# A deep-interest ranking network on one core: a sixth tile by address in two of three steps of history, a root on VectorE, categories as products of ones and zeros, and one norm for both parts of a layer

## The chip, the cores and the metric

The kernel runs on one core of one Trainium2 chip. A core has five engines, each with its own instruction queue: TensorE (PE; PEld is its loading of weights), VectorE (DVE), ScalarE (ACT), GpSimd (POOL) and SyncE (SP). SP, ACT and POOL also issue DMA transfers, and 16 DMA engines carry them. A profile writes SPq or ACTq for what such a queue issues. The metric is the time of one execution on the device in microseconds, less is better, taken as the median of several.

## The reference

There are 16,384 samples. For each, 200 items of history (`r_hist`, 200 x 16384 indices), one candidate item, one category and one user are looked up in tables of 64 float32 each.

```python
u = u_emb[user]; it = i_emb[item]; c = c_emb[cate]; h = i_emb[hist]
feat = concat([h, it, h - it, h * it])                  # 200 x 16384 x 256
a = dice(feat @ au_W1 + au_b1, au_alpha, axis=1)        # 36 units
cur = sum(w * h, axis=0), with w = a @ au_W2 + au_b2    # over the 200
z = dice(concat([u, it, c, cur]) @ W1 + b1, alpha1, axis=0)
z = dice(z @ W2 + b2, alpha2, axis=0)
return z @ W3 + b3
```

`dice(x)` is `x * (p + alpha * (1 - p))`, where `p` is the sigmoid of `x` normalised by its mean and variance. In the attention the mean runs over all samples of one step l of the history; in the head it runs over all samples.

## The kernel before

The 16,384 samples are 128 tiles of 128. Sixteen tiles make a column c, so one step l of the history has eight columns (ND = 8), and the program goes through k = 8 l + c. The 200 l are four passes of a loop whose body is 45 l written out, and then 20 l written out (`BODY`, `LPB`).

For each k, `fetch` (helper `gather`, L123) has POOL gather 16 tiles of rows, one indirect DMA of 128 rows each, into one of five buffers `rows`. Some tiles come another way. In the columns SIDES = (1, 3, 4, 5, 6, 7) the last tile is copied row by row with addresses: `load_addresses` (L145) brings the indices into `addr`, VectorE multiplies them by the row's bytes (L148), and `rows_by_address` loads 16 or 20 addresses at a time into registers (L293) and issues one DMA of 256 bytes for each row (L301), half on SP's queue and half on ACT's. The rows land in one of three tiles `side`, and the semaphore `landed` counts them. Column 5 (`SOMETIMES`) does so only when l is divisible by 3; otherwise POOL gathers that tile, with indices from `load_side_ids` (L142). So of three l one has six tiles by address (96 rows per k) and two have five (80 rows per k). `place` makes ACT wait for `landed`, clear it, and copy `side` into `rows` (L352).

The order within a k is written by hand in `step`: gathers for k; ACT's move of the units of k-2 out of `px` (L339); at the end of an l the moments (L363 on, with the square root on ACT at L170 and the reciprocal on VectorE at L171); ACT's sigmoid for k-9 (`gate`, L328; LAG = 9); `place` for k-1; the rows by address for k; then for k-1 VectorE's four transposes (L156) and TensorE's products, and VectorE's work for k-2, k-1 and k-9 (L344, L360, L331, L335, L336). A new l opens with the load of indices for the next one on SP (L136).

Ahead of the loop the candidate items are gathered by POOL, 128 gathers. After it, `head_fetch` gathers categories and users, 256 gathers; `head_layer` makes the first layer's products and moves its 64 and 16 units out separately (L486, L488). `head_moments` runs once for each part and once for the second layer, each with a square root on ACT; then come the two further layers and the output.

```python
for k in range(n * ND):
    l, c = divmod(k, ND)
    if c == 0 and l + 1 < end:
        load_hist_ids((l + 1) % IDX, l0 + l + 1)
```

Of the kernel before, what the change touches and what calls it, by code (L numbers as in the profile page):

```python
# [28 lines left out]
LOAD = 20  # L29
# [5 lines left out]
def din_kernel(  # L35
# [76 lines left out]
    ids = [make(f"ids{i}", P, NT, dt=I32) for i in range(3)]  # L112
# [17 lines left out]
    def load_ids(t, v):  # L130
        nc.sync.dma_start(t[:, :NC], columns(v))
        for s in range(NS):
            nc.sync.dma_start(t[:, NC + s : NC + s + 1], col(v[(NC + s) * P : (NC + s + 1) * P]))

# [9 lines left out]
    def load_addresses(i, l):  # L144
        nc.sync.dma_start(addr[i], r_hist[ds(l, 1), NC * P :])  # L145
# [21 lines left out]
    def scale_and_shift(mean, var, rstd, shift):  # L167
        n = mean.shape[0]
        std = small.tile([P, 1], F32, tag="std", name="std")
        nc.scalar.activation(std[:n], var, AF.Sqrt, bias=eps[:n])  # L170
        nc.vector.reciprocal(rstd, std[:n])  # L171
        nc.vector.scalar_tensor_tensor(shift, mean, -1.0, rstd, ALU.mult, ALU.mult)

    eps = make("eps", P, 1)
# [14 lines left out]
    def attention_weights():  # L189
        nc.vector.memset(eps, EPS)  # L190
# [45 lines left out]
    def head_weights():  # L236
# [3 lines left out]
        for e in range(2):  # L240
            for g in range(2):
                r, d = quarter(e, g), ts(e, S)
                nc.sync.dma_start(w1a[r, :, ts(g, ZA)], w1[d, :, :ZA])
                nc.sync.dma_start(w1b[r, :, ts(g, ZB)], w1[d, :, ZA:])
        for g in range(2):
            nc.sync.dma_start(w2a[ts(g, ZA), g * ZA : g * ZA + Z2], W2[:ZA])
# [20 lines left out]
    flat = i_emb.rearrange("v d -> (v d)").bitcast(U8)  # L267

# [4 lines left out]
    def tiles_by_address(l):  # L273

        round_, i = divmod(l, EACH)
        first = round_ * (EACH * (NS - 1) + 1) + i * (NS - 1) + (i > 0)
        return first, [j for j, c in enumerate(SIDES) if has_side(l * ND + c)]

    def rows_by_address(k):
        l, s = divmod(k, ND)  # L280
        first, tiles = tiles_by_address(l)
        n = len(tiles) * P // ND // 2
        loads = -(-n // LOAD)
        for i, (engine, issue) in enumerate(
            ((mybir.EngineType.SP, nc.sync), (mybir.EngineType.Activation, nc.scalar))
        ):
            r0, end = (2 * s + i) * n, (2 * s + i + 1) * n
            while r0 < end:
                many = min(end - r0, -(-n // loads))
                at0 = tiles[r0 // P] * P + r0 % P  # L290
                while tiles[(r0 + many - 1) // P] * P + (r0 + many - 1) % P != at0 + many - 1:
                    many -= 1
                _, at = nc.values_load_multi_w_load_instructions(  # L293
                    addr[l % 3][:, at0 : at0 + many],
                    engines=(engine,), min_val=0, max_val=ROW * (V - 1),
                    skip_runtime_bounds_check_because="the DMA checks the address against the table",
                )
                for r, a in enumerate(at, r0):
# [9 lines left out]

    def await_rows(m):
        if m in keys:  # L310
            fence = nc.scalar.wait_ge(landed[m % 3], 16 * P)
            tc.declare_fence(fence.ins, group=keys.pop(m))
            nc.scalar.sem_clear(landed[m % 3])

    def has_side(k):
        l, c = divmod(k, ND)
        return c in SIDES and (c != SOMETIMES or l % EACH == 0)
# [28 lines left out]
    def place(k):  # L346
        if has_side(k):
            l, c = divmod(k, ND)
            first, tiles = tiles_by_address(l)
            m = first + tiles.index(SIDES.index(c))  # L350
            await_rows(m)
            nc.scalar.copy(rows[k % ROWS][:, TD - 1], side[m % 3])  # L352
# [30 lines left out]
    def step(k, last=None):  # L383
# [12 lines left out]
        if has(k - LAG):  # L396
            gate(k - LAG)
        if has(k - 1):
            place(k - 1)
        if has(k):  # L400
            rows_by_address(k)
        if has(k - 1):
# [5 lines left out]
        if has(k - LAG):  # L408
# [3 lines left out]
    def steps(l0, n, end):  # L412
        for k in range(n * ND):
            l, c = divmod(k, ND)
            if c == 0 and l + 1 < end:
                load_hist_ids((l + 1) % IDX, l0 + l + 1)
                if (l + 1) % EACH:
                    load_side_ids((l + 1) % IDX, l0 + l + 1)
            if c == 2 and l + 1 < end:
                load_addresses((l + 1) % 3, l0 + l + 1)  # L420
            if c == 4 and l + 1 < end:
                scale_addresses((l + 1) % 3)
            step(k)

    with tc.manual_schedule():
        load_ids(ids[0], r_item)
        load_hist_ids(0, 0)
        load_addresses(0, 0)
        load_ids(ids[1], r_cate)
        load_ids(ids[2], r_user)  # L430
        nc.gpsimd.iota(lanes, pattern=[[1, P]], base=P, channel_multiplier=-1)
        attention_weights()
        for t in (*hT, *xs, *side, hm):
            nc.vector.memset(t, 0.0)
        for t in curT:
# [7 lines left out]
        scale_addresses(0)  # L443
        layer(px, [(blk_m, hm)])

        for c in range(ND + 1):
            if c < ND:
                for n in range(TD):
                    j = column(c, n)
                    gather(rows[c % ROWS], ids[0][:, j : j + 1], n, i_emb)  # L450
            if c:
                transpose(itT[c - 1], rows[(c - 1) % ROWS])
        nc.vector.memset(rows[-1 % ROWS], 0.0)
# [13 lines left out]
    def measure_head(i, j, t):  # L467
        for h in range(2):
            nc.vector.bn_stats(zst[i][:, 2 * j + h, :], t[:, ts(h, CH)])

    def head_fetch(k, j):
        c, u = divmod(j, 2)
        for n in range(TD):
            i = column(c, n)
            gather(rows[k % ROWS], ids[1 + u][:, i : i + 1], n, (c_emb, u_emb)[u])

    def head_layer(j):
        c, u = divmod(j, 2)
        if u == 0:
# [121 lines left out]
```

## Time and profile before

| | |
|---|---|
| median of 10 runs | 51,398.7 us (51,284.0 to 51,432.4) |
| the profiled execution | 51,313.9 us, span 51,312.1 us |
| POOL busy | 23,568.2 us (46%), 24,922 instructions |
| PE busy / PEld busy | 20,767.9 us (40%) / 8,519.6 us (17%) |
| DVE busy | 15,101.6 us (29%) |
| ACT busy | 4,417.8 us (9%) |
| rows by address | 68,288 on SP, 68,288 on ACT |
| gathers of history rows | 24,533 on POOL |

How to read it: issuing a DMA and loading a register are not counted as busy, so SP has no busy time of its own and ACT's is small; what these queues do is seen in the time line and in the waits. In a line of a group, the name left of the arrow is written and those right of it are read; after the bar stand the busy time, the mean of one instruction in ns, and the idle time ahead of them with what ended it. Times of POOL are rough.

### The profile page before, as it was taken

What the parts mean: (1) busy time and instruction counts of PE and PEld (TensorE: products, weight loads), DVE (VectorE), ACT (ScalarE), POOL (GpSimd) and SP (SyncE); (2) the same over time, 40 slices, a digit from 0 to 9 for tenths busy, and PEclk for the clock granted to TensorE, in tenths of its full rate; (3) what the DMA queues carried; (4) which work ended last, traced back from release to release, by engine and by line L of the source; (5) the groups of instructions that cost most, each with busy time, mean ns of one, the idle gap of its engine ahead of it and who ended that gap; (6) DMA issues with size and microseconds to landing.
All of it is one profiled execution on the core that took longest, in us unless ns stands there. A gap on an engine that the chain in (4) does not pass through costs nothing. (4 is left out here: it accounts for less than half of the span.)

```text
span 51312.1 us, 423966 instructions
## 1 busy us (share of the span) xinstructions
PE 20767.9 (40%) x38856; PEld 8519.6 (17%) x38856; DVE 15101.6 (29%) x18955; ACT 4417.8 (9%) x4941; POOL 23568.2 (46%) x24922
## 2 busy tenths in 40 slices
PE   3444444443444444444444444444444444434444
PEld 1111111111111111111111111111111111111111
DVE  2222222232222222222222222222222222222223
ACT  0000000000000000000000000000000000000001
POOL 5444444444444444444444444444444444444444
PEclk6666666676666666666676666666666666666667
DMA  1000000001000000000000000000000001000000
GB/s 19 18 17 17 18 17 17 17 17 18 17 18 17 17 18 17 17 17 17 17 18 17 17 17 18 17 17 17 17 17 18 17 17 18 17 17 17 18 17 17
DMA packets 1130924, 894.71 MB, mean 17 GB/s; under 512 B 729024, under 2 KB 729024, under 8 KB 1127896
## 3 DMA queue, kind: packets, MB, share of 16 engines
q0 software_dynamic: 797344, 818.07, 9.1%
q1 hardware_dynamic: 193112, 31.56, 0.3%
q10 hardware_dynamic: 137440, 17.76, 0.2%
q14 instruction: 2722, 22.30, 0.1%
q8 instruction: 306, 5.01, 0.0%
HBM read 865.10 MB, written 0.13 MB: 17 GB/s over the span
## 5 line engine op out<-in xcount | busy, mean ns | idle before, releaser
L123 POOL DMA_INDIRECT rows<-in_L_rec_i_emb,idx x24400 | 23078.7, 946 | 27336.3 <-DVE hT L156 19722.4
L161 PE MATMUL ph<-hT,unit 128*128 128x512 f32 x6404 | 5955.1, 1085 | 29876.1 <-DVE hT L156 29344.8
L335 DVE SCALAR_TENSOR_TENSOR wb<-wb,au_bias,hT 128x1024 f32<-128x1024 f32 x1609 | 2079.7, 1293 | 22888.2 <-remote 19196.7
L161 PEld LDWEIGHTS ph<-hT,unit 128*128 128x128 f32 x6404 | 1797.9, 311 | 32935.8 <-DVE hT L156 32140.7
L156 DVE STREAM_TRANSPOSE hT<-rows 64x512 f32<-64x512 f32 x6404 | 4516.7, 705 | 9048.8 <-ACT rows L352 8894.5
L339 ACT ACTIVATE xs<-px,au_bias 128x1024 f32<-128x1024 f32 x1602 | 1785.0, 1114 | 45250.8 <-issue 40079.8
L161 PE MATMUL px<-hT,blk_h 128*128 128x512 f32 x6404 | 4020.2, 715 | 403.2 <-ACT xs L339 211.1
L161 PE MATMUL px<-itT,blk_i 128*128 128x512 f32 x6404 | 3423.3, 617 | 0.0
L161 PE MATMUL wb<-xs,blk_x 128*128 128x512 f32 x6436 | 3294.0, 593 | 48.2 <-DVE curT L336 45.4
L161 PE MATMUL wb<-y,blk_p 128*128 128x512 f32 x6436 | 3294.6, 593 | 36.4 <-issue 19.5
L161 PE MATMUL px<-hm,blk_m 128*128 128x512 f32 x6408 | 3013.0, 592 | 71.1 <-remote 71.1
L344 DVE BATCH_NORM_STATS2 st<-xs 128x6 f32<-128x512 f32 x3204 | 2061.6, 686 | 2065.7 <-ACT xs L339 1611.2
L360 DVE TENSOR_TENSOR hm<-ph,itT 128x1024 f32<-128x1024 f32 x1601 | 1958.0, 1223 | 1725.2 <-PE ph L161 1162.2
L161 PEld LDWEIGHTS px<-hT,blk_h 128*128 128x128 f32 x6404 | 1601.0, 252 | 2890.7 <-issue 2528.8
L336 DVE TENSOR_TENSOR curT<-wb,curT 128x1024 f32<-128x1024 f32 x1609 | 1970.0, 1224 | 54.8
L331 DVE TENSOR_TENSOR y<-pg,xs 128x1024 f32<-128x1024 f32 x1609 | 1954.0, 1214 | 12.6 <-issue 10.3
L328 ACT ACTIVATE pg<-xs,sh,rs 128x1024 f32<-128x1024 f32 x1609 | 1934.1, 1202 | 28.4 <-DVE y L331 13.9
L161 PEld LDWEIGHTS px<-itT,blk_i 128*128 128x128 f32 x6404 | 1391.7, 217 | 1963.0 <-issue 1963.0
L161 PEld LDWEIGHTS wb<-xs,blk_x 128*128 128x128 f32 x6436 | 1224.1, 190 | 1593.7 <-issue 1544.4
L161 PEld LDWEIGHTS wb<-y,blk_p 128*128 128x128 f32 x6436 | 1224.7, 190 | 1582.5 <-issue 1559.2
L161 PEld LDWEIGHTS px<-hm,blk_m 128*128 128x128 f32 x6408 | 1218.0, 190 | 1606.1 <-issue 1533.8
L352 ACT COPY rows<-side 128x64 f32<-128x64 f32 x1068 | 251.3, 235 | 682.0 <-DMA side<-in_L_rec_i_emb 588.5
(155 smaller groups left out, 2148.1 us busy)
## 6 DMA issues: line engine op xcount, KB each, us to landing
side<-in_L_rec_i_emb SPq DMA_DIRECT2D x68288, 0.2 KB
side<-in_L_rec_i_emb ACTq DMA_DIRECT2D x68288, 0.2 KB
rows<-in_L_rec_i_emb,idx POOLq DMA_INDIRECT x24400
idx<-in_r_hist SPq DMA_DIRECT2D x200, 61.0 KB
addrs<-in_r_hist SPq DMA_DIRECT2D x200, 3.0 KB
sidx<-in_r_hist SPq DMA_DIRECT2D x133, 0.5 KB
rows<-in_L_rec_i_emb,sidx POOLq DMA_INDIRECT x133
rows<-in_L_rec_i_emb,ids POOLq DMA_INDIRECT x128
```

What stands on the lines that cost most here:

```text
L123: nc.gpsimd.indirect_dma_start(out=dst[:, n, :], out_offset=None, in_=table, in_offset=bass.IndirectOffsetOnAxis(ap=ids, axis=0),)
L156: nc.vector.transpose(by_tile(dst[ts(e, D)], i), of[ts(i, D), :, ts(e, S)])
L161: nc.tensor.matmul(dst[:, ts(i, CH)], lhsT, rhs[:, ts(i, CH)], start=(first and j == 0), stop=(last and j == len(pairs) - 1), skip_group_c ...
L328: nc.scalar.activation(pg, xs[k % XR], AF.Sigmoid, bias=shifts[i], scale=rstds[i])
L331: nc.vector.tensor_mul(y, pg, xs[k % XR])
L335: nc.vector.scalar_tensor_tensor(wb, wb, au_bias2, hT[k % LAG], ALU.add, ALU.mult)
L336: nc.vector.tensor_add(curT[k % ND], wb, curT[k % ND])
L339: nc.scalar.activation(xs[k % XR], px, AF.Identity, bias=au_bias)
L344: nc.vector.bn_stats(stats[l % 3][:, 2 * c + i, :], xs[k % XR][:, ts(i, CH)])
L352: nc.scalar.copy(rows[k % ROWS][:, TD - 1], side[m % 3])
L360: nc.vector.tensor_mul(hm, ph, itT[k % ND])
```

## The change

- Column 5 comes by address in two of three l (`MOST = 2`) in place of one, which makes 17 tiles by address in three l where there were 16. Registers are loaded with up to 24 addresses at a time (`LOAD`). In a step, ACT's share of the rows is issued in two parts, one ahead of its sigmoid and one behind it.
- The wait for landed rows, the clearing and the copy go from ACT to VectorE (`place_tile`).
- One over the root is found on VectorE by three steps of refinement from a shifted bit pattern; ACT has no square root any more.
- Six tiles of the candidate items, and five of the users, come by address as well (`ask_all`). Categories are not gathered: ahead of the loop, for each half column, VectorE compares category numbers with the numbers of 125 table rows at a time, TensorE multiplies the table by these ones and zeros, ACT moves the result out and stores it in DRAM, and the end loads it back by one DMA on SP per column.
- At the end the user and category parts are two calls of `head_layer` per column, both parts of the first layer are normalised in one pass (`start_moments`, `end_moments`), halves are moved out one by one, part of the scaling goes to ACT, and the first output is sent after the seventh column.

```diff
-LOAD = 20
+MOST = 2
+LOAD = 24
+SPLIT = 0.5
...
-        n = mean.shape[0]
-        std = small.tile([P, 1], F32, tag="std", name="std")
-        nc.scalar.activation(std[:n], var, AF.Sqrt, bias=eps[:n])
-        nc.vector.reciprocal(rstd, std[:n])
...
+        nc.vector.tensor_scalar_add(v, var, EPS)
+        nc.vector.tensor_single_scalar(h.bitcast(I32), v.bitcast(I32), 1, ALU.logical_shift_right)
+        nc.vector.tensor_scalar(
+            rstd.bitcast(I32), h.bitcast(I32), -1.0, float(0x5F375A00), ALU.mult, ALU.add
+        )
+        for _ in range(3):
+            if n == 1:
+                nc.vector.scalar_tensor_tensor(h, rstd, v, rstd, ALU.mult, ALU.mult)
...
+            nc.vector.tensor_scalar(h, h, -0.5, 1.5, ALU.mult, ALU.add)
+            nc.vector.tensor_mul(rstd, rstd, h)
...
-                nc.sync.dma_start(w1a[r, :, ts(g, ZA)], w1[d, :, :ZA])
-                nc.sync.dma_start(w1b[r, :, ts(g, ZB)], w1[d, :, ZA:])
+                for f in (slice(0, 2), slice(3, 4)):
+                    nc.sync.dma_start(w1a[r, f, ts(g, ZA)], w1[d, f, :ZA])
+                    nc.sync.dma_start(w1b[r, f, ts(g, ZB)], w1[d, f, ZA:])
...
+            nc.sync.dma_start(w1a[ts(g, D), 2, ts(g, ZA)], w1[:, 2, :ZA])
+            nc.sync.dma_start(w1b[ts(g, D), 2, ts(g, ZB)], w1[:, 2, ZA:])
...
-        first = round_ * (EACH * (NS - 1) + 1) + i * (NS - 1) + (i > 0)
+        first = round_ * (EACH * (NS - 1) + MOST) + i * (NS - 1) + min(i, MOST)
...
+    queues = ((mybir.EngineType.SP, nc.sync), (mybir.EngineType.Activation, nc.scalar))
+    def shares(n, s, split):
+        many = round(n * split)
+        runs = []
+        for r0, end in ((s * n, s * n + many), (s * n + many, (s + 1) * n)):
+            loads = -(-(end - r0) // LOAD)
+            at = [r0 + (end - r0) * i // loads for i in range(loads + 1)]
+            runs.append(list(zip(at, at[1:])))
+        return runs
...
+    def ask(queue, runs, first, tiles, at, table):
+        engine, issue = queues[queue]
...
+        for r0, end in runs:
             while r0 < end:
...
-                _, at = nc.values_load_multi_w_load_instructions(
-                    addr[l % 3][:, at0 : at0 + many],
-                    engines=(engine,), min_val=0, max_val=ROW * (V - 1),
+                _, loaded = nc.values_load_multi_w_load_instructions(
...
+    def ask_hist(k, queue, some):
+        l, s = divmod(k, ND)
+        first, tiles = tiles_by_address(l)
+        runs = shares(len(tiles) * P // ND, s, SPLIT)[queue]
+        ask(queue, runs[some], first, tiles, addr[l % 3], i_emb)
+    def ask_all(s, split, first, n, at, table):
+        for queue, runs in enumerate(shares(NS * P // ND, s, split)):
+            runs = [(r0, min(end, n * P)) for r0, end in runs if r0 < n * P]
+            ask(queue, runs, first, range(n), at, table)
...
         if m in keys:
-            fence = nc.scalar.wait_ge(landed[m % 3], 16 * P)
+            fence = nc.vector.wait_ge(landed[m % 3], 16 * P)
             tc.declare_fence(fence.ins, group=keys.pop(m))
-            nc.scalar.sem_clear(landed[m % 3])
+            nc.vector.sem_clear(landed[m % 3])
...
-        return c in SIDES and (c != SOMETIMES or l % EACH == 0)
+        return c in SIDES and (c != SOMETIMES or l % EACH < MOST)
...
-            m = first + tiles.index(SIDES.index(c))
-            await_rows(m)
-            nc.scalar.copy(rows[k % ROWS][:, TD - 1], side[m % 3])
...
+    def place_tile(k, m):
+        await_rows(m)
+        nc.vector.tensor_copy(rows[k % ROWS][:, TD - 1], side[m % 3])
+    def fetch_all(k, c, ids, table):
+        for n in range(TD - (c in SIDES)):
+            j = column(c, n)
+            gather(rows[k % ROWS], ids[:, j : j + 1], n, table)
...
                 moments((k - 2) // ND)
-        if has(k - LAG):
+        if has(k):
+            ask_hist(k, 0, slice(None))
+            ask_hist(k, 1, slice(0, 1))
+        if k - LAG not in weighed:
             gate(k - LAG)
+        if has(k):
+            ask_hist(k, 1, slice(1, None))
         if has(k - 1):
             place(k - 1)
-        if has(k):
-            rows_by_address(k)
...
-                if (l + 1) % EACH:
+                if (l + 1) % EACH >= MOST:
                     load_side_ids((l + 1) % IDX, l0 + l + 1)
...
+    def order_categories():
+        nc.scalar.dma_start(table, c_emb.rearrange("(b p) d -> p b d", p=PB))
+        for c in range(ND):
...
...
+    def spread_categories(q):
+        c, i = divmod(q, 2)
+        half = cs[c][ts(i, D)].rearrange("p n -> (p n)")
+        nc.scalar.dma_start(spread[q % SPREAD], half.partition_broadcast(PB))
+    def pick_categories(q):
+        for b in range(NB):
+            ones = xs[(q * NB + b) % XR][:PB]
+            nc.vector.tensor_scalar(
+                ones, spread[q % SPREAD], values[:PB, b : b + 1], None, ALU.is_equal
+            )
+            for g in range(2):
+                nc.tensor.matmul(
+                    bank[q % 8][ts(g, D)], table[:, b], ones[:, ts(g, CH)],
+                    start=b == 0, stop=b == NB - 1, skip_group_check=True,
+                )
+        nc.scalar.copy(
+            stages[q % 4].rearrange("p (n t) -> p n t", t=S),
+            bank[q % 8].rearrange("p (t n) -> p n t", n=TD),
+        )
+    def store_categories(q):
+        c, i = divmod(q, 2)
+        nc.scalar.dma_start(catT[c][:, ts(i, CH)], stages[q % 4])
...
     with tc.manual_schedule():
-        load_ids(ids[0], r_item)
+        nc.sync.dma_start(ids[0], columns(r_item))
+        load_addresses(2, r_item.rearrange("(o b) -> o b", o=1))
+        order_categories()
         load_hist_ids(0, 0)
...
+        nc.sync.dma_start(ids[1], columns(r_user))
         nc.gpsimd.iota(lanes, pattern=[[1, P]], base=P, channel_multiplier=-1)
+        for q in range(SPREAD - 1):
+            spread_categories(q)
...
+        scale_addresses(2)
+        nc.vector.memset(hm, 0.0)
+        for t in (*hT[SPREAD:], *curT[1:]):
+            nc.scalar.copy(t, hm)
+        for c in range(ND + 1):
+            if c < ND:
+                fetch_all(c, c, ids[0], i_emb)
+                ask_all(c, 0.56, -NS, NS, addr[2], i_emb)
+                for q in (2 * c, 2 * c + 1):
+                    pick_categories(q)
+                    if q + SPREAD - 1 < HALVES:
+                        spread_categories(q + SPREAD - 1)
+                    if q:
+                        store_categories(q - 1)
+            if c == 0:
+                attention_weights()
+                scale_addresses(0)
+            if c:
+                if c - 1 in SIDES:
+                    place_tile(c - 1, SIDES.index(c - 1) - NS)
+                transpose(itT[c - 1], rows[(c - 1) % ROWS])
+        store_categories(HALVES - 1)
...
+        for t in xs:
+            nc.scalar.copy(t, hm)
+        for t in (*hT[:SPREAD], *side, curT[0], rows[-1 % ROWS]):
             nc.vector.memset(t, 0.0)
...
+    def start_moments(key, j, n, i, same):
...
+        nc.vector.bn_aggr(mv[:, j], zst[i].rearrange("p c s -> p (c s)"))
+        nc.tensor.matmul(leading(pg, j, 1), same, mv[:, j, 0:1], start=True, stop=True)
+    def end_moments(key, sames):
...
+        for j, same in enumerate(sames):
+            nc.tensor.matmul(leading(wb, j, 1), same, dev[:, j : j + 1], start=True, stop=True)
...
+        scale_and_shift(mean, leading(wb, 0, n), rstd, shift)
...
+    def head_layer(c, pairs, first):
+        layer(px, [(w1a[:, f], t) for f, t in pairs], first=first, last=not first)
+        layer(ph[:S], [(w1b[:, f], t) for f, t in pairs], first=first, last=not first)
+    def evacuate(dst, src, bias, i, j):
         for h in range(2):
-            nc.vector.bn_stats(zst[i][:, 2 * j + h, :], t[:, ts(h, CH)])
+            nc.scalar.activation(dst[:, ts(h, CH)], src[:, ts(h, CH)], AF.Identity, bias=bias)
...
+    def head_units(c):
+        evacuate(za[c], px, b1a, 0, c)
...
-        steps(BODY, L - BODY, L - BODY)
+        steps(BODY, L - BODY, L - BODY, r_user.rearrange("(o b) -> o b", o=1))
...
+        weighed = set(range(-LAG, K - LAG))
+        for j in range(ND + 2):
+            if j < ND:
+                fetch_all(K + j, j, ids[1], u_emb)
+                if j == SIDES[-1]:
+                    gather(rows[(K + j) % ROWS], sidx[0], TD - 1, u_emb)
+                nc.sync.dma_start(category[j % 2], catT[j])
+            step(K + j, K - 1, weighed)
+            weighed.add(K + j - LAG)
             if j >= 2:
+                k = max(weighed) + 1
+                if k < K:
+                    gate(k)
+                    weights(k)
+                    weigh(k)
+                    weighed.add(k)
+            if j < ND:
+                ask_all(j, SPLIT, first, NS - 1, U, u_emb)
+            if 1 <= j <= ND:
+                c = j - 1
+                head_layer(c, ((2, category[c % 2]), (1, itT[c]), (3, curT[c])), True)
+                if c in SIDES[:-1]:
+                    place_tile(K + c, first + SIDES.index(c))
+                transpose(user[c % 2], rows[(K + c) % ROWS])
+                head_layer(c, ((0, user[c % 2]),), False)
+                head_units(c)
...
+        def dice(dst, z, norm, al1, al, parts=1, scalar=False):
...
+            for i in range(parts):
+                c = ts(i, CD // parts)
+                nc.scalar.activation(p[:, c], z[:, c], AF.Sigmoid, bias=norm[1], scale=norm[0])
+                if scalar:
+                    nc.scalar.activation(p[:, c], p[:, c], AF.Identity, bias=al, scale=al1)
+                else:
+                    nc.vector.tensor_scalar(p[:, c], p[:, c], al1, al, ALU.mult, ALU.add)
+                nc.vector.tensor_mul(dst[:, c], p[:, c], z[:, c])
...
+        start_moments("z", 0, 2, 0, same_a)
+        start_moments("z", 1, 2, 1, same_b)
+        na, nb = end_moments("z", (same_a, same_b))
...
+                evacuate(z2[c - 2], pz[(c - 2) % 4], bias2, 2, c - 2)
+        start_moments("z2", 0, 1, 2, same_a)
+        (n2,) = end_moments("z2", (same_a,))
+        def finish(g):
...
+                nc.vector.transpose(t[:, ts(i, CH)], pz[2 * g][:, ts(i, CH)])
...
+        for c in range(ND):
+            g, q = divmod(c, 4)
+            dice(curT[c], z2[c], n2, al12, al2, 2 if c == 0 else 1, c % 2 == 1)
+            layer(pz[2 * g], [(w3[:, q], curT[c])], first=q == 0, last=q == 3)
+            if c == ND - 2:
+                finish(0)
+                send(0, (nc.sync, nc.sync))
+        finish(1)
+        send(1, (nc.sync, nc.scalar))
```

## The prediction

> **What bounds the kernel now.** I read the page's busy times first, then the waits of the DMA queues, then the time line of SP's queue, then single stretches of it.
>
> The busy times point at POOL (46% of the span), yet POOL idles longer than it works, waiting for VectorE's transposes to free a buffer of rows. The costliest groups have it so:
>
> ```profile
> L123 POOL DMA_INDIRECT rows<-in_L_rec_i_emb,idx x24400 | 23078.7, 946 | 27336.3 <-DVE hT L156 19722.4
> ```
>
> The chain that ended last, and the waits of SP's queue (total us, times, longest), name another resource:
>
> ```profile
> SPq 16%; issue 12%; ACTq 3%; PE 0%; another core or an unknown queue 0%; ACT 0%; DVE 0%; DMA 0%; POOL 0%; DVEq 0%
> ...
> SPq L562 <- DVE res L553: 415.9, 2, 401.6
> SPq L293 <- remote: 75.6, 1, 75.6
> ...
> SPq L301 <- ACT xs L339: 3.6, 14, 0.6
> ```
>
> SP waits once before its first row (75.6 us), once at the end for the result (401.6), and in the 50.8 ms between for next to nothing: its queue never runs dry. The time line of SP (start, us, what) shows three successive l between the loads of L136 that open each:
>
> ```profile
> 19960.70 0.36 SPq L136 DMA_DIRECT2D idx<-in_r_hist  x1
> 19961.27 0.36 SPq L142 DMA_DIRECT2D sidx<-in_r_hist  x1
> 19963.00 64.99 SPq L301 DMA_DIRECT2D side<-in_L_rec_i_emb  x96
> 20028.28 0.23 SPq L145 DMA_DIRECT2D addrs<-in_r_hist  x1
> 20029.94 198.85 SPq L301 DMA_DIRECT2D side<-in_L_rec_i_emb  x288
> 20229.26 0.36 SPq L136 DMA_DIRECT2D idx<-in_r_hist  x1
> ...
> 20231.79 60.54 SPq L301 DMA_DIRECT2D side<-in_L_rec_i_emb  x80
> ...
> 20294.51 180.48 SPq L301 DMA_DIRECT2D side<-in_L_rec_i_emb  x240
> 20475.46 0.36 SPq L136 DMA_DIRECT2D idx<-in_r_hist  x1
> ...
> 20717.07 0.36 SPq L136 DMA_DIRECT2D idx<-in_r_hist  x1
> ```
>
> The first has six tiles by address (96 + 288 = 384 rows on SP) and takes 268.6 us; the others have five (320 rows) and take 246.2 and 241.6. Over 180 l, those at loop edges left out, the same marks are 269.1 us apart with six and 244.3 with five. **A sixth tile costs 24.8 us**, though it takes one gather from POOL.
>
> Where that goes, from four stretches of the same queue:
>
> ```profile
> 20029.94 11.46 SPq L301 DMA_DIRECT2D side<-in_L_rec_i_emb  x30
> 20042.12 15.55 SPq L301 DMA_DIRECT2D side<-in_L_rec_i_emb  x9
> ...
> 11477.55 70.22 SPq L301 DMA_DIRECT2D side<-in_L_rec_i_emb  x180
> ...
> 130.55 50.46 SPq L301 DMA_DIRECT2D side<-in_L_rec_i_emb  x20
> ...
> 190.87 49.00 SPq L301 DMA_DIRECT2D side<-in_L_rec_i_emb  x18
> ```
>
> Left alone, a row costs 0.325 us of queue (start to start); 180 rows and 8 loads of 20 addresses (1.451 us each) make 70.1, as seen at 11477. While a burst of POOL's gathers is under way the same pair of instructions takes 1.7 to 2.7 us, whether ScalarE's queue stands still (130: 20 rows) or issues too (190: 18). So an l is rows x 0.325, plus address loads, plus about 2 us of small DMAs, plus a toll per gather. With five: 320 x 0.325 = 104.0, 16 x 1.451 = 23.2, 2.0, and 123 gathers, which leaves 115.1, or 0.936 us each. With six: 124.8 + 24 loads of 16 addresses at 1.227 = 29.4, + 2.0 + 122 x 0.936 = 114.2, in all 270.4 against 269.1 measured. The sum holds.
>
> **The change, part by part.** The profiled execution took 51,313.9 us (span 51,312.1, 1.8 around it), 85 us under the median of the ten runs, 51,398.7.
>
> *Sixth tile in two of three l.* Six-tile l go from 67 to 134 (30 in each of four passes of 45, 14 in the last 20). Rows per step and queue stay 48 in these, 40 in the others. Each new one pays 24.8 us: 67 x 24.8 = +1,662. It also drops a load of one column of indices (L142), some 0.55 us of SP (start to start above): -35.
>
> *Address loads of 24.* 48 rows need two loads in place of three; 40 rows keep two of 20. No row shows 24 values. The recorded loads have medians of 0.591 us for 4 values, 1.227 for 16, 1.451 for 20: a straight line, 1.675 at 24. Two cost 3.35 where three cost 3.68; 8 steps save 2.6 us per six-tile l. Bounds: 24 priced like 16 saves 9.8, and no saving if the price grows so that two cost three. I take the line, since three rows lie on it: 134 x 2.6 = -349. Body: 1,662 - 349 - 35 = +1,278.
>
> *Root on VectorE, copy and wait moved from ScalarE to VectorE, ScalarE's rows split around its gate.* ScalarE loses per l two table loads (1.283 us each), the square root (0.29), five or six copies (0.235), clears, and its wait for the sum of moments (2.2 us). VectorE gains some twelve instructions of 0.16 us and the copies, about 3.5 us beside 74 busy in an l of 244; what hides them is VectorE's idle time waiting for ScalarE's copy (8,894 us in all). Behind the moved wait stand VectorE's transposes, then TensorE, POOL's buffer and, through the three side tiles, SP. The tile awaited is issued a step or more ahead, so I price it at nothing; were that cover gone, SP would stop. ScalarE's relief is priced at nothing too: it already waits for rows that SP shares (L352, 588 us), so SP ends last. *A rule weighed:* the Trainium skill, ScalarE: Activation LUTs, section What ACT_TABLE_LOAD costs, puts every switch at 2.66 us, with a drain behind the load. The trace has 1.283 for the load. By the page, 400 switches on the path would take 1,064 us off and the forecast would be about +200; by the rows of SP's waits they are worth nothing.
>
> *Start.* Before, SP begins rows at 113.7 and opens the second l at 495.6. Now item tiles come by address too. SP up to the same mark: 430 item rows (0.56 x 768) and 384 more, 814 x 0.325 = 265; 24 loads of 18 at about 1.34 and 16 at 1.675, 59; 122 + 122 gathers x 0.936 = 228, and 12 more for the first 80, which run without a break (50.46 / 20 = 2.5 us a row there); 30 small DMAs, 15; about 12 until addresses are there. That is 591: +95. Beside it TensorE does the categories: 16 halves x 16 calls x two records = 512 at 0.43 to 0.593 us, 220 to 304 us, and VectorE 128 comparisons at about 0.8. They fit beside the item rows (about 340 us by the same sum), with ScalarE's rows queued behind its copies of each half. Bounds: 0 if SP's waits of before absorb it, +200 if the products end last. Weights of the head need 12 more DMAs of 0.5: +6.
>
> *End.* Before, the last row is issued at 50,886.9 and 425 us follow, paced by 256 gathers. Now categories come ready-made; users need 123 gathers, of which POOL has two steps (32) done by then, as before, and 320 rows per queue: 104 + 14 x 1.675 = 23 + 91 x 0.936 = 85, so 212. Each category DMA on SP waits until TensorE has used the tile two steps older; user rows queue behind it. Then about 25 us for the last two columns. The final part, 89 us from the last activation of L486 on, loses table loads, one of two norms, and ScalarE's 10.6 us wait behind the first output: I take 74. Sum 311, -114. Bounds: -200 if the rows hide behind the gathers, 0 if those waits stretch each column to 40 us.
>
> **Sum:** 1,278 + 95 + 6 - 114 = **+1,265** on 51,313.9 gives 52,579; with the 85 us to the median, **52,664 us**, 2.5% slower. 0.2% (about 100 us) is what a measurement here can tell from none.
>
> **Rivals.**
> (a) *The queues get relief in the gather stretches.* If ScalarE's lighter queue lowered the toll per gather, all 24,300 would gain. It decides at 1,265 / 24,300 = 0.052 us, 6% of 0.936. At 0.1 off the time would be 52,664 - 2,430 = 50,230. Against it: SP's pace at 130 us without ScalarE is that at 190 with it. 7%.
> (b) *POOL is the bound,* as its 46% suggests: 67 gathers at 1.25 us less, -84 in the body, and +95 + 6 - 114 at the ends, so about 51,300, no change within 0.2%. The Trainium skill, Perfetto Trace Analysis, section Identifying the Most-Contended Engine, picks the engine of highest occupancy and would say this. The 24.8 us speak against it. 2%.
> (c) *VectorE's wait becomes SP's.* Three side tiles let SP lead by little over a step; if each of 1,134 tiles held SP for 1 us, +1,130: 53,800. The small waits now (3.6 us) speak against it. 9%.
> (d) *The forecast,* 82%; on its own 52,150 to 53,100, from loads priced like 20 (134 x 3.6 = -480) to no saving (+349), with about 100 at the ends either way.
>
> **Chances.** Slower by over 0.2%: (d) and (c), 0.91; within: 0.02; faster: (a), 0.07. The range that leaves out (a) and most of (c): 52,100 to 53,200.
>
> **What would show it.** Marks of L136's load about 266.5 us apart for six tiles and 244 for five; SP's waits in the body near nothing; two address loads per step at 1.6 to 1.7 us; VectorE waiting for landed rows; SP's second l opened near 590. I am wrong if six-tile l fall under about 257 us (then two thirds of them cost no more than one third did), if five-tile l shorten, or if SP shows waits on VectorE.

## The result and the profile after

The changed kernel takes 52,509.2 us (median of 8 runs, 52,471.0 to 52,543.0), the kernel before 51,384.9 on the same chip: a ratio of 1.0222 (95% interval 1.0213 to 1.0231), 2.2% slower. The forecast was 52,664. The profiled execution took 52,525.2 us, its span 52,523.4, so 1,211 us more than the span before; the terms below are held against that.

The runs of this study fell on several chips, called A to D here: A for the two kernels themselves, B, C and D for the experiments. (The record numbers B, C and D. For A it has no number; only the times of the kernel before tell it from the others.) Each ratio is against the kernel before on the same chip, and that kernel took 51,385 us on A, 51,007 on B, 51,470 to 51,484 on C, and 31,360 on D. The last number is no misprint, and the section on the experiments comes back to it.

The chain that ended last, of the changed kernel, and below it the waits of SP's queue (total us, times, longest). The shares of the chain add up to a tenth of the span only (about a third in the kernel before), so the waits are the stronger evidence:

```profile
SPq 6%; issue 4%; PE 0%; ACTq 0%; DVE 0%; another core or an unknown queue 0%; DMA 0%; ACT 0%; DVEq 0%
```

```profile
SPq L314 <- DVE rows L386: 137.8, 189, 1.5
SPq L712 <- DVE res L701: 115.1, 2, 112.8
SPq L253 <- DVE al L247: 85.5, 1, 85.5
SPq L322 <- DVE rows L386: 13.7, 61, 0.3
```

Rows by address are L322 now, address loads L314. SP's queue still hardly ever waits: VectorE copies 1,146 tiles, and all that SP waits for them in 51 ms is about 150 us, 1.5 at the longest. The two larger waits are at the start (L253, a weight of the head) and at the end (L712, the output).

The time line of SP's queue (start, us, what), between the index loads (L133 now) that open an l:

```profile
20083.88 0.36 SPq L133 DMA_DIRECT2D idx<-in_r_hist  x1
...
20346.65 0.36 SPq L133 DMA_DIRECT2D idx<-in_r_hist  x1
20348.61 57.56 SPq L322 DMA_DIRECT2D side<-in_L_rec_i_emb  x80
...
20408.35 185.67 SPq L322 DMA_DIRECT2D side<-in_L_rec_i_emb  x240
20594.54 0.36 SPq L133 DMA_DIRECT2D idx<-in_r_hist  x1
...
20859.12 0.36 SPq L133 DMA_DIRECT2D idx<-in_r_hist  x1
```

The middle l has five tiles (80 + 240 rows) and takes 247.9 us; those on either side have six and take 262.8 and 264.6. Over 180 l the marks are 264.1 and 264.4 us apart with six tiles and 246.0 with five (269.1 and 244.3 before). Two of three l now pay for six.

The costliest groups, two lines of them (busy us, mean ns, then the idle time ahead and what ended it):

```profile
L125 POOL DMA_INDIRECT rows<-in_L_rec_i_emb,idx x24400 | 23018.7, 943 | 28704.0 <-DVE hT L153 20757.4
L386 DVE COPY rows<-side 128x64 f32<-128x64 f32 x1146 | 221.0, 193 | 8892.9 <-DMA side<-in_L_rec_i_emb 8860.0
```

POOL idles more than before (28,704 us, 27,336 before). The wait for landed rows stands on VectorE as the change says, 8,860 us of it. SP loses next to nothing by it, as its own waits above show: the tiles that VectorE waits for are the ones that SP and ScalarE are still issuing.

Where the 1,211 us come from, by three marks of SP's queue (second l opened, last row of the history, end of the span):

| | before | after | difference | forecast |
|---|---|---|---|---|
| to the opening of the second l | 495.6 | 710.7 | +215 | +95, and +6 for weights |
| from there to the last row of the history | 50,391.0 | 51,493.2 | +1,102 | +1,278 |
| from there to the end | 425.5 | 319.5 | -106 | -114 |
| sum | | | +1,211 | +1,265 |

### The profile page after: what moved, and what is told of

Read it like the earlier page. It is cut to its first block, busy times and chain, and to the rows that moved or that the text cites. A ratio compares the mean times of both kernels' runs of the same rounds, so it can differ in the third digit from the quotient of the medians.

```text
span 52523.4 us, 445332 instructions
## 1 busy us (share of the span) xinstructions
PE 21803.1 (42%) x39376; PEld 8784.8 (17%) x39376; DVE 15806.6 (30%) x22426; ACT 3821.9 (7%) x3321; POOL 23314.2 (44%) x24716
## 5 line engine op out<-in xcount | busy, mean ns | idle before, releaser
L158 PE MATMUL wb<-y,blk_p 128*128 128x512 f32 x6440 | 3795.9, 674 | 5102.4 <-DVE y L363 4506.8
L158 PE MATMUL wb<-xs,blk_x 128*128 128x512 f32 x6440 | 3578.1, 639 | 12.6 <-DVE curT L368 12.6
L386 DVE COPY rows<-side 128x64 f32<-128x64 f32 x1146 | 221.0, 193 | 8892.9 <-DMA side<-in_L_rec_i_emb 8860.0
L158 PEld LDWEIGHTS wb<-y,blk_p 128*128 128x128 f32 x6440 | 1337.1, 215 | 6972.5 <-DVE y L363 4743.3
```

The source lines that it names most:

```text
L158: nc.tensor.matmul(dst[:, ts(i, CH)], lhsT, rhs[:, ts(i, CH)], start=(first and j == 0), stop=(last and j == len(pairs) - 1), skip_group_c ...
```

## The experiments

**Theory:** SP's queue, and ScalarE's beside it, issue the rows and never wait, so every row (0.325 us), every address load and a toll per gather of POOL make up the time. **Rivals:** relief of ScalarE counts too; POOL is the bound; a wait moved between engines is what counts.

**1. One sixth tile in three l, all else changed (after_most1, chip B).**

```diff
-MOST = 2
+MOST = 1
```

> The changed kernel with the sixth tile in one of three l again (MOST = 1), all else as changed. If SP's queue sets the time: 67 l fall from 264.3 to about 246 us, 67 x 18.3 = 1,226, and one index load comes back in each, +35, so 52,509 - 1,191 = about 51,320, within 0.3% of the kernel before. If instead VectorE's new wait, the root or the start carry the loss, the time stays above 52,000. If POOL were the bound, 67 more gathers at 1.25 us make it 52,590.

Measured: 50,865.8 us, ratio 0.9974 (0.9965 to 0.9984). So it is the sixth tile that makes the changed kernel slower; without it, the rest of the change is 0.26% faster than the kernel before.

**2. The sixth tile alone (before_most2, chip B).**

```diff
-        first = round_ * (EACH * (NS - 1) + 1) + i * (NS - 1) + (i > 0)
+        first = round_ * (EACH * (NS - 1) + 2) + i * (NS - 1) + min(i, 2)
...
-        return c in SIDES and (c != SOMETIMES or l % EACH == 0)
+        return c in SIDES and (c != SOMETIMES or l % EACH < 2)
...
-                if (l + 1) % EACH:
+                if (l + 1) % EACH >= 2:
```

> The kernel before with nothing but the sixth tile in two of three l. SP's queue: 67 x 24.8 - 35 = +1,627, about 53,010, six-tile l at 269 and five-tile l at 244. POOL's gathers as the bound: 51,300. If the change's other parts carry the loss, it stays near 51,385.

Measured: 52,608.3 us, ratio 1.0318 (1.0300 to 1.0335), which is +1,601 us against the 1,627 of the prediction's terms (1,662 - 35). Marks: 266.4 and 267.5 us with six tiles, 242.7 with five: 24.3 us for the tile. The largest term is confirmed by itself.

**3. Address loads of at most 20 (after_load20, chip B).**

```diff
-LOAD = 24
+LOAD = 20
```

> The changed kernel with 20 addresses at most in one load, so 48 rows need three loads of 16 again. If loads lie on SP's path at the durations recorded (1.227 us for 16 values, 1.675 for 24): 134 l x 8 steps x 0.33 = +354, about 52,860, and six-tile l near 266.9. If the six-tile l became shorter than forecast because ScalarE was relieved, the same +354. If the longer load saved more than its own duration, six-tile l go back to 269.1: 134 x 4.8 = +643, about 53,150. If loads are hidden: 52,510.

Measured: 52,535.4 us, ratio 1.0301 (1.0284 to 1.0319), so 0.79% of 51,385, some 400 us, above the changed kernel's ratio (which is from chip A; by the ends of the two intervals 270 to 545 us). On the same chip B the marks of the l divisible by 3, which have six tiles in both kernels, are 265.4 us apart here and 262.3 with loads of 24 (after_most1): 3.1 us each, where the prediction had 2.6. (The other six-tile l, 265.9 us here, have no like in after_most1.) In the body of the changed kernel a load of 24 has a median of 1.675 us, the value on the line. Why the saving is above the line's was not tried. That a third load is also a few more instructions in stretches where each is held up by gathers would explain it, but that is argued only.

**4. Wait, clearing, copy and root back on ScalarE (after_scalar, chip B).**

```diff
-            fence = nc.vector.wait_ge(landed[m % 3], 16 * P)
+            fence = nc.scalar.wait_ge(landed[m % 3], 16 * P)
...
-            nc.vector.sem_clear(landed[m % 3])
+            nc.scalar.sem_clear(landed[m % 3])
...
-        nc.vector.tensor_copy(rows[k % ROWS][:, TD - 1], side[m % 3])
+        nc.scalar.copy(rows[k % ROWS][:, TD - 1], side[m % 3])
...
+        std = small.tile([P, n], F32, tag=f"std{n}", name="std")
+        nc.scalar.activation(std[:p], var, AF.Sqrt, bias=eps[:p])
+        nc.vector.reciprocal(rstd, std[:p])
```

> The changed kernel with the wait, the clearing, the copy and the square root back on ScalarE. If ScalarE's relief is worth nothing, since SP ends last: within 100 us of 52,509. If the body came out 141 us under the forecast because ScalarE was relieved: about 52,650. If each switch of tables with its drain lay on the path (400 x 2.66 us): about 53,570. If the wait on VectorE costs SP time, it gets faster than 52,400.

Measured: 61,608.8 us, ratio 1.2079 (1.2059 to 1.2099). None of the expectations foresaw a loss of this size. The waits of SP's queue, and those of ScalarE, of this kernel:

```profile
SPq L311 <- ACTq L332: 10500.1, 834, 41.7
```

```profile
ACT rows L375 <- DMA side<-in_L_rec_i_emb: 9519.8, 1131, 9.3
```

SP waits 834 times for ScalarE to clear a side tile (L332). In the changed order ScalarE issues all its rows of step k ahead of the copy for step k-1, so the tile that SP needs comes free only after rows that are issued for a later one. SP's lead over three side tiles is gone, and its waits of 10,500 us cover the 9,500 that the kernel lost against the changed kernel's ratio of 1.0222. So the mechanism of rival (c) is real, on ScalarE with this order; VectorE is spared it.

**5. The same, with the copy ahead of ScalarE's rows, as in the kernel before (after_order, chip C).**

```diff
-            ask_hist(k, 1, slice(0, 1))
...
-        if has(k):
-            ask_hist(k, 1, slice(1, None))
         if has(k - 1):
             place(k - 1)
+        if has(k):
+            ask_hist(k, 1, slice(None))
+        if has(k - 1):
             turn(k - 1)
```

> As the run that put the wait, the clearing, the copy and the square root back on ScalarE, but with the copy placed ahead of all of ScalarE's rows of the step, as before the change. Theory one (SP's queue sets the time; ScalarE's relief is worth nothing, and the 9.5 ms of that run came only from the wait standing behind the rows of the next step): ratio to before 1.022, between 1.018 and 1.027, marks of SP 264 us apart with six tiles and 246 with five, SP's waits for ScalarE near nothing. Theory two (the relief of ScalarE is worth something; by the figure of 2.66 us that the Trainium skill, ScalarE: Activation LUTs, What ACT_TABLE_LOAD costs, gives, 400 switches are 1,064 us): ratio about 1.043. Theory three (the wait on ScalarE is dear wherever it stands): ratio 1.1 to 1.2.

Measured: 52,753.1 us, ratio 1.0248 (1.0233 to 1.0264). The waits of SP's queue for ScalarE's clearing:

```profile
SPq L311 <- ACTq L332: 22.8, 2, 15.5
```

10,500 us of waiting became 23. The place of the wait was worth 9 ms. What this edit takes from the changed kernel (the engine that waits, root and copies, and also the split of ScalarE's rows around its sigmoid, since all of them now stand behind it) is worth 0.26%: about 134 us, and between 10 and 260 by the ends of the two intervals (the two ratios are from different chips). The marks of one chip agree: on C six-tile l are 266.0 and 266.7 us apart here and 264.5 and 265.1 in after_pick1 (below), whose body is that of the changed kernel, and five-tile l 244.9 here and 246.6 there. Six-tile l get 1.6 us longer by the edit and five-tile l 1.7 shorter, which makes 134 x 1.6 - 66 x 1.7 = 102 us. That is the relief of ScalarE, which the prediction priced at nothing.

With the figure of the Trainium skill (ScalarE: Activation LUTs, What ACT_TABLE_LOAD costs), 2.66 us for a switch, 400 switches would be an estimated 1,064 us if all of them lay on the path. This kernel has 417 table loads of 1.283 us and loses some 100 to 134 us by all that the edit puts back, so most of that time is not on the path here.

**6. Products of the first of eight parts of the category table only (after_pick1, chip C).**

```diff
-        for b in range(NB):
+        for b in range(1):
```

> Leaves out part of the computation: the categories are compared with and multiplied by the first of the eight parts of their table only, so 7/8 of the comparisons and products of the start are gone; nothing else changes. Theory one (the products end last at the start): SP's second l opens 90 to 120 us earlier than the 710 us of the changed kernel, near 600, SP's wait of 85.5 us ahead of the weights of the head goes below 10, and the time falls by 90 to 120 us, about 0.2%. Theory two (the item rows and gathers end last, the products lie beside them): the second l opens between 680 and 715 us and the time stays within 0.05%.

Measured: 52,588.6 us, ratio 1.0213 (1.0199 to 1.0227): no difference from the changed kernel that these intervals show. Against the trace of the changed kernel on chip A, SP's wait of 85.5 us ahead of the head's weights is gone and the first l opens 72 us earlier (357.9, 430.2 with all products). But the second l opens at 668.8, only 42 us earlier. The first l now holds 153 gathers instead of 127; the 26 others had been issued ahead of it, half of them while SP waited. So the products did end last, as theory one has it, but SP's wait hid gathers, and 26 of them come back as toll (an estimate: 26 x 0.92 = 24 of the 30 us between 72 and 42); less than half of the 90 to 120 us was to be had.

**7. Half of the gathers left out (after_half, chip C).**

```diff
-        for n in range(TD - has_side(k)):
+        for n in range(8):
```

> Leaves out part of the computation: of each column of the history POOL gathers the first 8 tiles only, so an l has 64 gathers in place of 122 or 123; the rows by address stay. Theory one (SP's queue sets the time and each gather costs it about 0.92 us): an l shortens by 58.3 x 0.92 = 54 us on average, from 258 to about 204 us, in all about 10,800 us less, a time near 41,500; six-tile and five-tile l still 18 to 22 us apart. Theory two (the 115 us that rows and address loads leave open are SP's own or another engine's, and gathers only happen beside them): an l stays between 245 and 258 us, the time above 49,500.

Measured: 38,936.5 us in one run (51,470 before). The time line of SP's queue, a five-tile l:

```profile
15103.72 0.36 SPq L133 DMA_DIRECT2D idx<-in_r_hist  x1
15105.69 41.51 SPq L322 DMA_DIRECT2D side<-in_L_rec_i_emb  x80
...
15149.39 129.03 SPq L322 DMA_DIRECT2D side<-in_L_rec_i_emb  x240
15278.94 0.36 SPq L133 DMA_DIRECT2D idx<-in_r_hist  x1
```

The same 320 rows took 247.9 us above and take 175.2 here. On average five-tile l go from 246.0 to 174.0 and six-tile l from 264.3 to 198.4. Rows and loads taken off (129.2 and 153.6 us by the prediction's terms), 44.8 us are left in both, 0.70 us for each of 64 gathers. With 15 or 16 gathers in a row it was 0.92. So the gathers do cost SP its time, as theory one says, but the toll is not a constant: each of the gathers taken out had cost 1.14 to 1.22 us, close to the 1.25 us at which POOL issues them. The traces show why: a run of gathers slows the queue only some microseconds after its start. In the changed kernel one instruction of SP's rows takes 0.19 us on average in the first 2 us of a run, 0.42 after 4 to 6, 0.72 after 8 to 10 and 1.2 from 14 on; in after_half, whose runs end after 10 us, 0.18, 0.46 and 0.67.

**8. Hardly any rows by address (after_s1, chip C).**

```diff
-SIDES = (1, 3, 4, 5, 6, 7)
-SOMETIMES = 5
+SIDES = (7,)
+SOMETIMES = 7
...
-MOST = 2
+MOST = 1
...
-            loads = -(-(end - r0) // LOAD)
+            loads = max(1, -(-(end - r0) // LOAD))
```

> The changed kernel with one column in place of six that has a tile by address, in one of three l: 128 or 127 gathers in each l, hardly any rows by address. Theory one (SP and ScalarE's queues set the time because of the rows by address, and POOL would do the work alone at the 1.25 us per gather of its unbroken bursts): an l takes 160 us, 200 l take 32,000, with 1,500 to 2,000 at the ends about 33,800. Theory two (in the stretches of gathers every engine's instructions come slowly, TensorE's 48 and VectorE's of a step among them): 190 us per l or more, 39,500 or above. Theory three (POOL waits for VectorE's transposes, 20,848 us in all, for a cause other than the rows by address): no gain, above 48,000.

Measured: 42,240.0 us, ratio 0.8207 (0.8194 to 0.8219): 18% faster than the kernel before, on a chip where a tile by address costs SP so much. It did not reach POOL's own pace, 33,800; an l takes 206 us on average, as theory two has it. A step of its time line (gathers and weight loads left out):

```profile
20017.80 1.88 PE L158 MATMUL px<-hm,blk_m 128*128 128x512 f32 x4
...
20022.09 1.02 PE L158 MATMUL wb<-y,blk_p 128*128 128x512 f32 x2
20034.60 1.11 ACT L371 ACTIVATE xs<-px,au_bias 128x1024 f32<-128x1024 f32 x1 [27.16 <-issue]
20035.62 1.20 ACT L360 ACTIVATE pg<-xs,sh,rs 128x1024 f32<-128x1024 f32 x1
20038.81 1.29 DVE L367 SCALAR_TENSOR_TENSOR wb<-wb,au_bias,hT 128x1024 f32<-128x1024 f32 x1 [22.60 <-remote]
```

TensorE's products for `px` end at 20,019.7 by the record, ScalarE moves them out at 20,034.6, and VectorE takes `wb` 15.7 us after its last product; POOL gathered without a break from 19,995 to 20,034 and stood still for the ten microseconds after. Of VectorE's waits in the whole run this one leads:

```profile
DVE wb L367 <- remote: 18717.0, 800, 53.0
```

So in long runs of gathers other engines' steps come late too, not only SP's. What holds them the profile does not name ("remote"), and no run here tests it.

**9. The same edit of the kernel before (before_s1), and two and three tiles in every l of the changed kernel (after_s2, after_s3), all on chip D.**

```diff
 # after_s2
-SIDES = (1, 3, 4, 5, 6, 7)
-SOMETIMES = 5
+SIDES = (3, 7)
+SOMETIMES = 3
...
-MOST = 2
+MOST = 3
 # after_s3
-SIDES = (1, 3, 4, 5, 6, 7)
+SIDES = (2, 5, 7)
...
-MOST = 2
+MOST = 3
```

> The kernel before with one column in place of six that has a tile by address, in one of three l, nothing else of the change. Theory one (what sets the time with hardly any rows by address lies in the stretches of gathers and not in the parts that the change moved): ratio to before 0.82 to 0.83, within 1% of the same edit of the changed kernel (0.8207). Theory two (with SP's queue out of the way ScalarE's square root and its table loads come on the path, 2 loads of 1.283 us, the root and its wait of 2.2 us, some 5 us of each l, 1,000 us in all): ratio 0.84. Theory three (the lower time of the changed kernel with few tiles by address needs the change's other parts): ratio above 0.87.

> The changed kernel with two tiles by address in every l (columns 3 and 7). SP's queue by the terms of the prediction: 128 rows x 0.325 = 41.6, 8 loads of 16 at 1.227 = 9.8, 2.0, 126 gathers x 0.92 = 116, in all 169 us of an l. Theory one (the larger of two limits counts, SP's queue or the other one, 206 us with a third of a tile): 200 to 206 us of an l, 41,000 to 42,300 in all, ratio 0.80 to 0.82. Theory two (every tile by address adds its share, on the straight line from 206 us at a third of a tile to 250 at five and a third: 9 us a tile): 221 us, about 45,200, ratio 0.88.

> The changed kernel with three tiles by address in every l (columns 2, 5 and 7). SP's queue: 192 rows x 0.325 = 62.4, 8 loads of 24 at 1.675 = 13.4, 2.0, 125 gathers x 0.92 = 115, in all 193 us of an l. Theory one (the larger limit counts): 195 to 206 us of an l, 40,000 to 42,300 in all, ratio 0.78 to 0.82. Theory two (every tile adds its share): 230 us, about 47,000, ratio 0.915.

Measured on chip D, where the kernel before takes 31,359.9 us: before_s1 32,476.2, ratio 1.0347 (1.0309 to 1.0386); after_s2 31,976.5, ratio 1.0188 (1.0150 to 1.0226); after_s3 31,736.2, ratio 1.0112 (1.0074 to 1.0149). All expectations were for a chip like A, B and C and say nothing here, and whether the edit of before_s1 makes the kernel before faster on such a chip was not run; the traces say a good deal. SP's queue in a stretch in which POOL gathers without a break, first in the changed kernel on chip A, then in after_s3 on chip D:

```profile
20327.71 11.83 SPq L322 DMA_DIRECT2D side<-in_L_rec_i_emb  x9
```

```profile
15009.16 10.75 SPq L322 DMA_DIRECT2D side<-in_L_rec_i_emb  x27
```

9 rows in 11.8 us on one chip, 27 in 10.8 on the other. On D there is no toll. Then POOL sets the time; what it waits for, in after_s3, its first three lines:

```profile
POOL rows L125 <- issue: 7274.8, 23856, 0.3
POOL rows L125 <- DMA rows<-in_L_rec_i_emb,idx: 315.4, 1035, 0.3
POOL rows L125 <- DVE rows L386: 81.8, 183, 11.2
```

The first two are the 0.3 us between one gather and the next; the third has the longest pause, 11.2 us. While it gathers the history, POOL pauses for longer than a microsecond only four times, once between each two stretches of the written-out loop. From the first of these gathers to the last it takes 31,899 us in before_s1 (25,533 gathers), 31,494 in after_s2 (25,200) and 31,258 in after_s3 (25,000), so 1.249 to 1.250 us a gather and 159.5, 157.5 and 156.3 us an l. There every tile by address saves 1.25 us an l. The changed kernel itself was not run on D. An estimate from these rows: 67 gathers fewer are 84 us, 0.27%, so the sixth tile, which costs 1,600 us on B, could help there. It is an upper bound: with six tiles SP's own rows and loads take 153.6 us of an l, and POOL's 122 gathers 152.4.

**10. Three tiles in every l, on a chip that pays the toll (after_s3_again, chip C).** The edit is that of after_s3.

> The same kernel as after_s3 (three tiles by address in every l), since the kernel before took 31,360 us on the chip of that call and 51,000 to 51,500 on the others, so that the ratios of that call answer another question. If the kernel before takes about 51,400 again (SP's queue pays for every gather): theory one (the larger of the two limits counts, SP's queue at 193 us of an l or the other one at 202 to 206): ratio to before 0.77 to 0.82; theory two (every tile by address adds its share to the 206 us of a third of a tile): 230 us of an l, ratio 0.915. If it takes about 31,400: ratio 1.011 again, 156 us of an l, the 125 gathers at 1.25 us each.

Measured: 48,236.5 us, ratio 0.9378 (0.9362 to 0.9393); an l takes 229 to 238 us. Theory one falls, and theory two, the straight line, was still 2.5% too low. A line of VectorE's waits:

```profile
DVE y L363 <- ACT pg L360: 17344.8, 923, 43.9
```

VectorE waits 17,345 us for ScalarE's sigmoid (5,672 in the changed kernel). ScalarE has 24 rows in each step ahead of its sigmoid, as in a six-tile l of the changed kernel, but POOL's runs of gathers are longer (about 29 us on average, 19 there). From 16 us after the start of a run one instruction of ScalarE's rows takes 1.1 to 1.5 us, the sigmoid comes late, and TensorE, the transposes and POOL's buffers wait in turn. So the two limits seem not to be apart but to meet in ScalarE's queue; this is read from the waits, and no run moves those rows to test it. Of the kernels run that leave nothing out, after_s1 is the fastest on a chip with the toll, and the kernel before on chip D. Only the kernel before and that of after_s3 ran on both kinds of chip, and each is the better one on one of them.

## Why the prediction was right

**What bounds the kernel.** Right on the chip it was made for: SP's queue waits about 150 us in the body, the sixth tile alone gives +1,601 us (1,627 by the terms), and taking it back gives 0.9974. That the total came within 54 us of its forecast (1,211 against 1,265) is in part luck: the body came out 176 us under its terms, the start 114 over and the end 8 over.

**The toll.** The prediction took 0.936 us for every gather. That is a mean over runs of one length, and it held because the change leaves that length nearly as it was (15.6 gathers in a run before, 16.5 after). Where runs get shorter, each gather saved is worth 1.14 to 1.22 us (experiment 7).

**Sixth tile and address loads, +1,278.** Measured +1,102. A newly six-tile l costs 264.3 - 244.3 = 20.0 us more (21.7 by the terms, 24.8 - 2.6 - 0.5), an old one is 4.8 us cheaper (2.6), a five-tile l 1.7 dearer (0): 67 x 20.0 - 67 x 4.8 + 66 x 1.7 = 1,131 over 200 l; the 1,102 us of the table hold all but the first l. Two terms were mis-sized. The saving by loads of 24 is 3.1 us of a six-tile l and not 2.6 (experiment 3), some 67 us in all, though the load itself costs what the line said. And the relief of ScalarE, put at nothing, saves 1.6 us of a six-tile l and costs 1.7 of a five-tile one (experiment 5), a saving of some 100 us in all. Measured on chips B and C, these figures make 4.7 of the 4.8 us of an old six-tile l on A, and all of the five-tile l's 1.7. On chip B the last is smaller: the five-tile l of after_load20 and before_most2 are 0.7 us apart (243.4, 242.7). Which of the parts that experiment 5 puts back does it was not tried.

**Root, copy and wait at nothing.** SP waits near nothing for VectorE, as argued, but ScalarE's relief is worth about 0.2 to 0.3%. What the prediction did not weigh is that the move of the wait is needed for the new order of ScalarE's rows: had the wait stayed on ScalarE, its place among them would have decided about 9 ms. The prediction looked at the engine, and the price hung on what stands ahead of the wait in that engine's queue.

**Start, +95.** Measured +215, 15 us beyond the upper bound of +200. The bound's cause, products that end last, is there (the wait of 85.5 us), but taking nearly all the products away gave 42 us only. What the sum left out: up to the second mark POOL has issued 306 gathers, where the sum has 244 and 12 us more, the toll of 256 in all; 50 x 0.936 = 47 us. With the 6 us for weights that is 95 + 6 + 42 + 47 = 190; some 25 us stay open. In the start the 24 address loads of 18 values took 1.7 us (median) and up to 4.54 on SP, 53 us together, where the prediction had 1.34 and 32; part of that may be the toll again, so it is not added here.

**End, -114.** Measured -106. The user rows took 193 us (212 forecast) and what follows the last of them 126 (25 + 74 = 99).

**Rivals.** (a) Relief of ScalarE is there but small: some 100 us over 24,300 gathers are 0.004 us each (experiment 5), where 0.052 would have decided. (c) 150 us of waits in place of 1,130. (b) POOL as the bound is wrong on A, B and C and right on D for the kernels traced there. The Trainium skill (Perfetto Trace Analysis, Identifying the Most-Contended Engine) picks the engine of highest occupancy: POOL in both cases, at 44% in the changed kernel on A, where it does not bind, and at 75% in after_s3 on D, where it does.

## What to carry to other kernels

When a queue that issues DMAs hardly ever waits, count its instructions and price them in the stretch where they run, not where they run free: here one row costs 0.33 us or 1.8 us depending on what POOL does beside it. Moving a wait is priced by what stands ahead of it in its new queue. And a balance between two ways to fetch the same data can turn round from one chip to another: run both ends of it on more than one chip before settling it.

## What was not expected of the hardware

On chips A, B and C every instruction of SP's queue slows while POOL gathers, not only DMAs. Time from the start of one instruction of SP's rows to the start of the next, means over 5 to 25 ms of each trace, stretches over 5 us left out; "in gathers" means that at least six gathers started in the 8 us before it, "free" that none did:

| | register move, free | in gathers | DMA of one row, free | in gathers |
|---|---|---|---|---|
| before (A) | 0.062 us | 0.943 us | 0.268 us | 0.946 us |
| changed kernel (A) | 0.061 | 0.905 | 0.269 | 0.911 |
| after_most1 (B) | 0.061 | 0.898 | 0.268 | 0.914 |
| after_s3_again (C) | 0.063 | 1.021 | 0.268 | 1.037 |
| after_s3 (D) | | 0.073 | | 0.268 |

A register move transfers no data, and takes 0.9 us in a run of gathers. POOL's gathers look alike on all chips (0.943 to 0.946 us each, one in 1.249 to 1.252). Instructions come by DMA themselves (23.6 MB on the instruction queue q14 in the changed kernel), but a packet of them takes 0.455 us on A and 0.467 on D (medians), so the packets are not slower where the toll is paid. Why the other engines' instructions are held back during gathers on A, B and C and not on D stays open. D served for one series of runs only, so no run here tells whether it is the chip itself or something else that was different then.
